# One multiplication for two buckets: pairing one-hot buffers in a four-layer graph network kernel

## The chip, the cores and the metric

The kernel runs on one core of a Trainium2 chip. The metric is the time of one execution on the device in microseconds (us). The engines of a core run side by side, each through its own queue in order: PE multiplies matrices (PEld is its loading of weights), DVE is the vector engine, ACT the scalar engine, POOL the general one, and SP issues transfers. They wait for each other through semaphores.

## The reference

Sixteen graphs of 1024 nodes with 128 features each go through four layers. The adjacency is sparse: an entry is there with a chance of about 1.6%, plus the diagonal. Each layer adds to `x`:

```python
x = x + L0(relu(layernorm(x)), adj, adj)   # degrees, neighbours by adj transposed, linear, relu
x = x + L1(relu(layernorm(x)), adj)        # mean of neighbours, linear, leaky relu
x = x + L2(relu(layernorm(x)), adj)        # scores on edges, two rounds
x = x + L3(relu(layernorm(x)), adj)        # attention by softmax
```

The change is in L2. A round of it, of which there are two, is this (`x` is a local name here):

```python
a = x @ We1[l, :D];  b = x @ We1[l, D:]
h = relu(a[:, :, None, :] + b[:, None, :, :] + be1[l])
scores = sigmoid((h @ We2[l]).squeeze(-1) + be2[l])
messages = (adjacency * scores) @ x
# then a two-layer update of [x, messages], a residual, a layer norm
```

Scores are needed only where the adjacency isn't zero, and the kernel computes them only there.

## The kernel before, in words

The 1024 nodes are 8 tiles of 128. A *bucket* is a pair of tiles (t, u): 28 off the diagonal and 8 on it. The edges of a bucket get *slots*: 320 in a bucket off the diagonal, 480 on it, laid out in blocks of 128 (3 or 4 blocks; `ck`). Buckets are worked in 9 *groups* of four (`GROUPS`, Q = 4): two groups of diagonal buckets, seven of others. A group off the diagonal goes in both directions (`nd` = 2), a diagonal one in one.

For each bucket `build` makes four one-hot matrices in 8-bit floats: `on` and `om` (node by slot, for gathering) and their transposes `onT` and `omT` (slot by node, for scattering). It does so from counts, ranks and comparisons: `far` on ACT (line 816), `on` on DVE (line 820), a transpose through PE (line 829), `onT` on ACT (line 861), a product with the ranks on PE (line 865), `omT` by a comparison on DVE (line 869), another transpose, `om` on ACT (line 877). They live in a pool of their own, `hot`, in buffers handed round: 8 per kind for diagonal buckets, 30 for the other 28. They are built once per graph and read in both rounds.

A round of L2 (`round`) takes the groups in turn. For each bucket and direction `gather` fetches both nodes' features into slots by one-hot products (line 1008, PE), and splits the relu into a high half on ACT (line 1024) and a low half on DVE (line 1025). `dots` reduces them to one score per slot (line 1041). At the end of a group, `ends` applies a tanh to all of its scores, and then, beside the next group's gathers, `scores` turns them so that slots lie on partitions (line 1074), splits them into two 16-bit halves held in one 32-bit word (`u`, lines 1079 to 1086), and multiplies every bucket's `onT` or `omT` with them: line 1098, one DVE instruction per bucket and direction, eight in a group off the diagonal, four in a diagonal one. The results, `val`, already lie two buckets to a buffer. `scatter` then multiplies the other transposed one-hot with `val` on PE (line 1120), four parts to a group, two (bucket, direction) products to a part off the diagonal; DVE multiplies the result with the adjacency (`upd`, line 1128), and `messages` sums it up on PE (line 1137).

Three streams of work are interleaved: the rounds of graph b (`main`), the last steps of graph b-1 (`last`, with the attention layer), and the first layers of graph b+1, at whose end stands its `build` (`first`). `weave` writes the program in the order of each stream's progress in estimated microseconds; a scheduler then sets the order on each engine by dependencies and priority. A one-hot buffer of graph b is free for graph b+1 once its last reader in the second round is done: a scatter or a multiplication of line 1098.

Of the kernel before, what the change touches and what calls it, by code (L numbers as in the profile page):

```python
# [11 lines left out]
FP8 = mybir.dt.float8e4  # L12
I32 = mybir.dt.int32
AF = mybir.ActivationFunctionType
OP = mybir.AluOpType
# [36 lines left out]
def tile_four_gnn_layers(  # L52
# [24 lines left out]
    P = 128  # L77
# [6 lines left out]
    J = P // G  # L84
    Q = T // NH
# [96 lines left out]
    def flat(t):  # L182
        return t.rearrange("p t d -> p (t d)")
# [266 lines left out]
    def slots(t, s):  # L450

        return (C_DIAG, CK_DIAG) if t == s else (C_OFF, CK_OFF)
# [77 lines left out]
    class Edges:  # L530
# [271 lines left out]
            nc.vector.tensor_reduce(top[:, 1:2], end[:, no:], axis=AX.X, op=OP.max)  # L802
            nc.vector.tensor_tensor(self.most, self.most, top, op=OP.max)

        def hot_tile(self, what, t, u, n, name):

            kind, bufs = ("d", T + MORE_DIAG) if t == u else ("o", len(OFF) + MORE_OFF)
            return self.hot.tile(
                [P, n], FP8, tag=f"{what}{kind}", name=f"{what}_{name}", bufs=bufs
            )  # L810

        def rows_hot(self, s, t, u, name):
# [22 lines left out]
        def build(self, s, has, name):  # L835

            s.on, s.onT, s.om, s.omT = {}, {}, {}, {}
            yield None  # L840
            for g, grp in enumerate(GROUPS):
                c, ck = slots(*grp[0])

                pr = self.a.one(f"pr_{name}_{g}").rearrange("p (k m) -> p k m", m=P)
                for i, tu in enumerate(grp):
                    b = INDEX[tu]
                    nc.tensor.matmul(
                        pr[:, i], self.low2, s.cnt[:, b : b + 1].to_broadcast([P, P]),
                        start=True, stop=False,
                    )  # L850
                    nc.tensor.matmul(pr[:, i], has[:, b], self.tri2, start=False, stop=True)
                rank = self.work.tile([P, Q, P], F16, tag="rank", name=f"rank_{name}_{g}")
                nc.scalar.activation(rank, pr, AF.Copy)
                yield 0.5
                for i, (t, u) in enumerate(grp):
                    nm = f"{name}_{t}_{u}"
                    on = self.rows_hot(s, t, u, nm)
                    yield 0.1
                    pn = self.turned(on, ck, f"pn_{nm}")
                    onT = self.hot_tile("onT", t, u, ck * P, nm)  # L860
                    nc.scalar.activation(onT, pn[:, : ck * P], AF.Copy, saturate=False)  # L861
                    yield 0.35
                    pq = self.a.one(f"pq_{nm}").rearrange("p (k m) -> p k m", m=P)
                    for k in range(ck):
                        nc.tensor.matmul(  # L865
                            pq[:, k], on[:, k * P : (k + 1) * P], rank[:, i], start=True, stop=True
                        )
                    omT = self.hot_tile("omT", t, u, ck * P, nm)
                    nc.vector.tensor_tensor(
                        omT.rearrange("p (k m) -> p k m", m=P), pq[:, :ck],  # L870
                        self.odd[t == u][:, :, None].to_broadcast([P, ck, P]),
                        op=OP.is_equal, saturate=False,
                    )
                    yield 0.35
                    pm = self.turned(omT, ck, f"pm_{nm}")
                    om = self.hot_tile("om", t, u, c, nm)
                    nc.scalar.activation(om, pm[:, :c], AF.Copy, saturate=False)  # L877
                    s.on[t, u], s.om[t, u] = on, om
                    s.onT[t, u], s.omT[t, u] = (
                        v.rearrange("p (k n) -> p k n", n=P) for v in (onT, omT)  # L880
                    )
                    yield 0.35
# [73 lines left out]
        class Group:  # L956
# [110 lines left out]
            def scores(self):  # L1067


                path, ck, per, name = self.path, self.ck, self.per, self.name  # L1070
                row = path.srow
                pt = path.bank("sc", f"pt_{name}")
                for k in range(ck):
                    nc.tensor.transpose(pt[:, k * P : (k + 1) * P], row[:, k * P : (k + 1) * P], ident)
                pt = pt[:, : ck * P].rearrange("p (c r) -> p c r", r=G)[:, :, :per]
                u = path.work.tile([P, CK_DIAG * J * 2], F32, tag="u", name=f"u_{name}")
                u = u[:, : ck * J * per]
                u2 = u.bitcast(F16).rearrange("p (c r h) -> p c r h", r=per, h=2)
                nc.scalar.activation(u2[:, :, :, 1], pt, AF.Copy, scale=S_SCALE)
                nc.vector.scalar_tensor_tensor(  # L1080
                    u2[:, :, :, 0], pt, S_SCALE, u2[:, :, :, 1], op0=OP.mult, op1=OP.subtract
                )
                if not self.diag:

                    again = u2[TAIL:, (ck - 1) * J :]
                    nc.vector.tensor_copy(again[:, :, :, 1], again[:, :, :, 0])
                u = u.rearrange("p (k g r) -> p k g r", g=J, r=per)
                self.val, self.ps = {}, [None] * self.nd
                for d in range(self.nd):
                    for i in range(Q):  # L1090
                        if i % 2 == 0:
                            pair = flat(path.m.scratch(f"val_{name}_{d}_{i}")).rearrange(
                                "p (d c n) -> p d c n", d=2, n=P
                            )
                        j = i * self.nd + d
                        right = (self.s.omT if d else self.s.onT)[self.grp[i]]
                        v = u[:, :, j % J, j // J : j // J + 1]
                        nc.vector.tensor_tensor(  # L1098
                            pair[:, i % 2, :ck], right[:, :ck], v.to_broadcast([P, ck, P]), op=OP.mult
                        )  # L1100
                        self.val[d, i] = pair[:, i % 2]

            def scatter(self, part):

# [281 lines left out]
    with ExitStack() as stack:  # L1386
        path = Edges(stack)
# [16 lines left out]
    with tc.If(full > 0):  # L1404
        with ExitStack() as stack:
            path = Pairs(stack)
# [36 lines left out]
```

## Time and profile before

| | |
|---|---|
| time, median of 3 runs | 5404.78 us (5400.31 to 5408.11) |
| span of the profiled run | 5411.4 us |
| granted clock of PE, mean share | 0.978 |
| HBM traffic | 446.44 MB read, 100.66 MB written, 101 GB/s |
| DVE, line 1025 (hid) | 1010.0 us in 2048 instructions |
| DVE, line 1128 (upd) | 349.0 us in 512 |
| DVE, line 869 (omT off the diagonal) | 247.6 us in 448 |
| PE idle until ACT's onT (line 861), before line 865 | 39.1 us, 55 times |
| PE idle until DVE's omT (line 869), before line 829 | 27.9 us, 39 times |

How to read it: the page gives the busy time of every engine, that is the time covered by at least one of its instructions; a group of instructions has its busy time, the mean length of one, and the idle time of the engine just before them with what ended it. The chain of work that ended last is followed back from the last instruction, from each to what released it; an engine's share of the chain is the part of the span in which the end depended on it. Instructions of one engine overlap a little, so starts and lengths are to be read apart.

### The profile page before, as it was taken

How to read it: one execution, taken by the hardware profiler on the slowest of the kernel's cores; microseconds unless marked ns; L12 is line 12 of the kernel's file. 1: busy time of each engine (PE TensorE's matmuls, PEld its weight loads, DVE VectorE, ACT ScalarE, POOL GpSimd, SP SyncE). 2: the span in 40 equal slices, each digit the busy share in tenths (PEclk: the TensorE clock that was granted, in tenths of full speed). 3: DMA queues.
4: the chain of work that ended last, by engine and by line, in shares of the span. 5: the costliest groups of instructions: out<-in, count | busy, mean ns of one | idle time of the engine just before them, and what ended most of it. 6: DMA issues, size and time to landing. Idle time of an engine off the chain costs nothing.

```text
span 5411.4 us, 113484 instructions
## 1 busy us (share of the span) xinstructions
PE 5012.4 (93%) x45109; PEld 3743.8 (69%) x45109; DVE 4288.8 (79%) x10567; ACT 3055.3 (56%) x6790; POOL 176.5 (3%) x137
## 2 busy tenths in 40 slices
PE   5999999999999999999999999999999999999986
PEld 4666767767776767767777677677767677677664
DVE  4776787877879788797877878778797787978876
ACT  4556464655646556465565656556465564655533
POOL 0000000000000000000000000000000000000000
PEclk8999999999999999999999999999999999999998
DMA  6242425243252423424234242432424334243121
GB/s 182 66 138 87 120 60 150 79 128 103 76 149 64 136 92 99 133 67 124 92 112 121 61 142 87 122 106 76 147 67 137 91 96 136 67 128 92 53 62 47
DMA packets 740139, 554.56 MB, mean 102 GB/s; under 512 B 32272, under 2 KB 686352, under 8 KB 739600
## 3 DMA queue, kind: packets, MB, share of 16 engines
q1 hardware_dynamic: 734496, 545.58, 33.6%
q8 instruction: 356, 5.83, 0.5%
q10 hardware_dynamic: 5104, 1.65, 0.1%
q14 instruction: 183, 1.50, 0.1%
HBM read 446.44 MB, written 100.66 MB: 101 GB/s over the span
## 4 chain that ended last, share of the span: by engine, by line
PE 61%; DVE 20%; ACT 10%; DMA 4%; POOL 2%; issue 2%; SPq 0%; ACTq 0%; POOLq 0%; DVEq 0%
PE pre L1008 15%; PE p L1120 7%; DVE val L1098 6%; PE nb L289 6%; PE msg L1137 5%; PE h L343 4%; PE hp L507 3%; PE bb L297 3%; PE sc L1041 3%; DVE hid L1025 3%; DMA at<-in_adj_dram 3%; PE pq L865 2%; PE pn L829 2%; POOL st L242 2%; ACT hid L1024 2%
## 5 line engine op out<-in xcount | busy, mean ns | idle before, releaser
L1024 ACT ACTIVATE hid<-pre 128x320 f16<-128x320 f32 (+1 forms) x2048 | 922.2, 456 | 713.5 <-PE pre L1008 679.5
L1025 DVE SCALAR_TENSOR_TENSOR hid<-pre,hid 128x320 f16<-128x320 f32 (+1 forms) x2048 | 1010.0, 505 | 262.7 <-ACT hid L1024 245.8
L1008 PEld LDWEIGHTS <-part 128*128 128x128 f16 x8192 | 752.7, 99 | 429.3 <-issue 211.4
L1008 PE MATMUL pre<-on,part 128*128 128x320 fp8e4 (+1 forms) x4096 | 966.6, 311 | 42.5 <-DVE hid L1025 32.3
L1008 PE MATMUL pre<-om,part 128*128 128x320 fp8e4 (+1 forms) x4096 | 979.0, 312 | 0.0
L1098 DVE TENSOR_TENSOR val<-onT,u 128x384 f32<-128x384 fp8e4 (+1 forms) x1152 | 603.3, 580 | 3.6
L1137 PE MATMUL msg<-upd,xf 128*128 128x128 f32 (+3 forms) x3008 | 591.8, 320 | 0.0
L1120 PE MATMUL p<-val,omT 128*128 128x128 f16 x6528 | 532.7, 219 | 31.6 <-DVE val L1098 27.2
L1120 PEld LDWEIGHTS <-omT 128*128 128x128 fp8e4 x6528 | 433.4, 96 | 109.6 <-issue 37.1
L1098 DVE TENSOR_TENSOR val<-omT,u 128x384 f32<-128x384 fp8e4 x896 | 442.7, 549 | 0.0
L1137 PEld LDWEIGHTS msg<-upd,xf 128*128 128x128 f32 x3008 | 411.6, 191 | 17.6 <-DVE upd L1128 0.9
L877 ACT ACTIVATE om<-pm 128x320 fp8e4<-128x320 f32 (+1 forms) x576 | 268.6, 466 | 274.5 <-PE pm L829 270.1
L1128 DVE SCALAR_TENSOR_TENSOR upd<-p,adj 128x512 f32<-128x512 f32 x512 | 349.0, 682 | 80.7 <-PE p L1120 76.7
L1120 PE MATMUL p<-val,onT 128*128 128x128 f16 x4480 | 370.9, 220 | 1.4 <-DVE upd L1128 1.4
L861 ACT ACTIVATE onT<-pn 128x384 fp8e4<-128x384 f32 (+1 forms) x576 | 298.4, 518 | 106.4 <-PE pn L829 98.4
L1062 ACT ACTIVATE srow<-sc,be_s,down 128x128 f32<-128x128 f32 (+2 forms) x512 | 256.3, 540 | 163.3 <-PE sc L1041 162.3
L507 PE MATMUL hp<-wh,e 128*128 128x129 f32 x2048 | 331.1, 287 | 16.7 <-DVE e L503 16.7
L1120 PEld LDWEIGHTS <-onT 128*128 128x128 fp8e4 x4480 | 305.2, 97 | 49.5 <-issue 14.9
L507 PEld LDWEIGHTS hp<-wh,e 128*128 128x128 f32 x2048 | 279.9, 195 | 51.5 <-issue 24.0
L1041 PE MATMUL sc<-hid,slide 128*32 128x320 f16 (+1 forms) x4096 | 272.4, 320 | 29.9 <-DVE hid L1025 28.5
L820 DVE TENSOR_SCALAR on<-far,wid 128x384 fp8e4<-128x384 f16 (+1 forms) x576 | 238.6, 427 | 60.0 <-PE pre L1008 52.2
L816 ACT ACTIVATE far<-iota_off,mid 128x384 f16<-128x384 f16 x448 | 275.6, 629 | 11.8 <-DVE on L820 11.3
(217 smaller groups left out, 8122.0 us busy)
## 6 DMA issues: line engine op xcount, KB each, us to landing
at<-in_adj_dram SPq DMA_DIRECT2D x128, 512.0 KB, 4.1
ct<-in_adj_dram SPq DMA_DIRECT2D x128, 512.0 KB, 4.5
adjT<-tn SPq DMA_DIRECT2D x128, 512.0 KB, 5.3
l<-adjT SPq DMA_DIRECT2D x128, 512.0 KB, 4.3
adj<-adjT SPq DMA_DIRECT2D x256, 256.0 KB, 3.5
a<-adjT SPq DMA_DIRECT2D x128, 384.0 KB, 3.2
adj<-adjT SPq DMA_DIRECT2D x448, 64.0 KB, 2.2
adj<-adjT SPq DMA_DIRECT2D x192, 128.0 KB, 2.9
```

Of the source, the lines that this page charges most:

```text
L289: nc.tensor.matmul(ps, mat[:, k], z[:, k], start=(k == 0), stop=(k == T - 1))
L507: nc.tensor.matmul(sums[:, t], e[:, i, t * P : (t + 1) * P], wh[:, k + i, : D + 1], start=False, stop=True, skip_group_check=True,)
L816: nc.scalar.activation(far[:, : ck * P], self.iota[t == u][:, : ck * P], AF.Abs, bias=s.mid[:, i : i + 1])
L861: nc.scalar.activation(onT, pn[:, : ck * P], AF.Copy, saturate=False)
L1008: nc.tensor.matmul(pre[:, :c], path.parts[node // Q][:, k, node % Q, v], hot[:, :c], start=(hot is on and k == 0), stop=(hot is om and k = ...
L1024: nc.scalar.activation(hid[:, 0, :c], pre[:, :c], AF.Relu)
L1025: nc.vector.scalar_tensor_tensor(hid[:, 1, :c], pre[:, :c], 0.0, hid[:, 0, :c], op0=OP.max, op1=OP.subtract)
L1041: ins = nc.tensor.matmul(self.sc[g * G : (g + 1) * G, : self.c], self.path.slide[:, self.l, G - 1 - r : 2 * G - 1 - r], self.hid[self.done ...
L1098: nc.vector.tensor_tensor(pair[:, i % 2, :ck], right[:, :ck], v.to_broadcast([P, ck, P]), op=OP.mult)
L1120: nc.tensor.matmul(self.ps[d][:, i], left[:, k], halves[:, k, :, h], start=(k, h) == terms[0], stop=(k, h) == terms[-1],)
L1128: nc.vector.scalar_tensor_tensor(upd, self.ps[d], S_SCALE, self.adj[:, d * Q : (d + 1) * Q], op0=OP.add, op1=OP.mult,)
L1137: nc.tensor.matmul(self.msg[h][:, (lo - h * Q) * P : (hi - h * Q) * P], self.xf[mb // Q][:, mb % Q], up, start=False, stop=True, skip_grou ...
```

## The change

`onT` and `omT` of two neighbouring buckets of a group get one buffer of twice the width (the `pair`), with half as many buffers in the pool; both buffers are taken at the first bucket of the two. As `val` already lay in pairs, one DVE instruction can now multiply the scores of two buckets into the one-hots of both: a loop over pairs takes the place of the loop over buckets, and the score operand gets one more dimension, with a step from one bucket's column to the next one's. What each bucket computes is unchanged. It is for having half as many DVE instructions of this kind, each of twice the size.

```diff
-        def hot_tile(self, what, t, u, n, name):
+        def hot_tile(self, what, t, u, n, name, both=1):
             kind, bufs = ("d", T + MORE_DIAG) if t == u else ("o", len(OFF) + MORE_OFF)
             return self.hot.tile(
-                [P, n], FP8, tag=f"{what}{kind}", name=f"{what}_{name}", bufs=bufs
+                [P, both * n], FP8, tag=f"{what}{kind}", name=f"{what}_{name}", bufs=bufs // both
             )
...
-                    onT = self.hot_tile("onT", t, u, ck * P, nm)
+                    if i % 2 == 0:
+                        pair = {
+                            what: self.hot_tile(what, t, u, ck * P, nm, 2).rearrange(
+                                "p (i k n) -> p i k n", i=2, n=P
+                            )
+                            for what in ("onT", "omT")
+                        }
+                        s.pairs[t, u] = pair
+                    onT, omT = (flat(pair[what][:, i % 2]) for what in ("onT", "omT"))
...
-                    omT = self.hot_tile("omT", t, u, ck * P, nm)
...
-                for d in range(self.nd):
-                    for i in range(Q):
-                        if i % 2 == 0:
-                            pair = flat(path.m.scratch(f"val_{name}_{d}_{i}")).rearrange(
-                                "p (d c n) -> p d c n", d=2, n=P
-                            )
-                        j = i * self.nd + d
-                        right = (self.s.omT if d else self.s.onT)[self.grp[i]]
-                        v = u[:, :, j % J, j // J : j // J + 1]
+                nd = self.nd
+                for d in range(nd):
+                    for i in range(0, Q, 2):
+                        pair = flat(path.m.scratch(f"val_{name}_{d}_{i}")).rearrange(
+                            "p (i c n) -> p i c n", i=2, n=P
+                        )
+                        right = self.s.pairs[self.grp[i]]["omT" if d else "onT"]
+                        j = i * nd + d
+                        v = u[:, :, j % J : j % J + nd + 1 : nd, j // J : j // J + 1]
                         nc.vector.tensor_tensor(
-                            pair[:, i % 2, :ck], right[:, :ck], v.to_broadcast([P, ck, P]), op=OP.mult
+                            pair[:, :, :ck], right, v.rearrange("p k i o -> p i k o").to_broadcast(
+                                [P, 2, ck, P]
+                            ), op=OP.mult,
                         )
-                        self.val[d, i] = pair[:, i % 2]
+                        for h in range(2):
+                            self.val[d, i + h] = pair[:, h]
```

## The prediction

> **What bounds the kernel now.** I read the page first: the shares of the engines, then the chain that ended last, then the costliest groups.
>
> ```profile
> PE 5012.4 (93%) x45109; PEld 3743.8 (69%) x45109; DVE 4288.8 (79%) x10567; ACT 3055.3 (56%) x6790; POOL 176.5 (3%) x137
> ...
> PE 61%; DVE 20%; ACT 10%; DMA 4%; POOL 2%; issue 2%; SPq 0%; ACTq 0%; POOLq 0%; DVEq 0%
> PE pre L1008 15%; PE p L1120 7%; DVE val L1098 6%; PE nb L289 6%; PE msg L1137 5%; PE h L343 4%; PE hp L507 3%; PE bb L297 3%; PE sc L1041 3%; DVE hid L1025 3%; DMA at<-in_adj_dram 3%; PE pq L865 2%; PE pn L829 2%; POOL st L242 2%; ACT hid L1024 2%
> ...
> L1098 DVE TENSOR_TENSOR val<-onT,u 128x384 f32<-128x384 fp8e4 (+1 forms) x1152 | 603.3, 580 | 3.6
> L1120 PE MATMUL p<-val,omT 128*128 128x128 f16 x6528 | 532.7, 219 | 31.6 <-DVE val L1098 27.2
> ...
> L1098 DVE TENSOR_TENSOR val<-omT,u 128x384 f32<-128x384 fp8e4 x896 | 442.7, 549 | 0.0
> ```
>
> The matrix engine (PE) carries 61% of the chain, the vector engine (DVE) 20%. Neither is the bound throughout. Line 1098, which the change rewrites, is 603.3 + 442.7 = 1046 us of DVE in 2048 instructions, and 6% of the chain, that is some 325 us of 5411: about a third of what it runs counts, two thirds lie under other work. It waits for almost nothing (3.6 us of idle before it). The matrix engine waits for it rarely: 27.2 us in all.
>
> How it runs is in the timeline of DVE, in the part of a batch where the next batch's one-hots are built (columns: start, length, instructions; several alike are merged):
>
> ```profile
> 2707.11 0.17 DVE L1086 COPY u<-u 64x8 f16<-64x8 f16 x1
> 2707.32 0.56 DVE L869 TENSOR_TENSOR omT<-pq,odd_off 128x384 fp8e4<-128x384 f32 x1
> 2707.79 1.95 DVE L1098 TENSOR_TENSOR val<-onT,u 128x384 f32<-128x384 fp8e4 x4
> 2709.66 1.96 DVE L1098 TENSOR_TENSOR val<-omT,u 128x384 f32<-128x384 fp8e4 x4
> 2711.54 0.55 DVE L869 TENSOR_TENSOR omT<-pq,odd_off 128x384 fp8e4<-128x384 f32 x1
> 2712.00 0.88 DVE L1025 SCALAR_TENSOR_TENSOR hid<-pre,hid 128x320 f16<-128x320 f32 x2
> ```
>
> Eight multiplications stand in one block of 3.83 us (2707.79 to 2711.62), and the hid of line 1025, on which the gathers of PE depend, comes after them. That block is what is on the chain. The reader is to see the starts: four instructions take 2709.66 - 2707.79 = 1.87 us, 468 ns each, although one lasts 549. Each overlaps the next by some 80 ns, so the price of one more instruction is less than its length suggests. The table of windows tells where DVE is short:
>
> ```profile
> 2675.00:2700.00 25.00, 24.13 (x257) 18.89 (x256) 24.24 (x57) 16.70 (x42) 0.00 (x0) 1.00 0.22 65
> 2700.00:2725.00 25.00, 24.65 (x262) 18.46 (x260) 23.74 (x57) 19.24 (x46) 0.00 (x0) 1.00 0.22 65
> ...
> 2450.00:2475.00 25.00, 24.86 (x235) 19.23 (x233) 18.99 (x43) 14.52 (x34) 0.00 (x0) 1.00 0.50 145
> 2475.00:2500.00 25.00, 24.83 (x229) 19.21 (x227) 18.26 (x45) 12.66 (x30) 0.00 (x0) 1.00 0.57 172
> ```
>
> (PE, weight loads, DVE, ACT.) In the build part both PE and DVE are nearly full, 24.1 to 24.7 and 23.7 to 24.2 of 25 us; in the other part PE is full and DVE has a quarter free.
>
> **What the Trainium skill says.** "VectorE: DVE Perf Modes", section on the TRN2 errata, gives a float32 tensor_tensor (N + 151) / 0.96 ns: 557 for 384 elements, 691 for 512. The trace agrees (549 and 684). The same section says that the latency is exposed between instructions, and that one large tile pays it once: this is what the change is after. Its table of perf modes holds a float32 tensor_tensor at one element per cycle, so merging can win only the fixed part; (684 - 550) / 128 = 1.05 ns per element here agrees. "Perfetto Trace Analysis" warns in its opening that matmul busy time says little since matmuls are pipelined. Here too: one line-1120 matmul lasts 219 ns but 6528 of them are busy for 532.7 us, 82 ns each. So 93% is no proof that PE is full.
>
> **The change part by part.**
> - *Removed:* 1024 of the 2048 instructions of line 1098. 224 groups of slots off the diagonal go from 8 to 4, 64 diagonal ones from 4 to 2. The elements stay.
> - *Cost of a merged one:* the row of line 501, a DVE pass over 128x768 float32, has a mean of 952 ns, and 550 + 384 x 1.05 = 953 agrees: I take 952 (the skill's formula would give 957). For 1024 elements 684 + 512 x 1.05 = 1222. Start to start: 468 + 384 x 1.05 = 871 (or 468 + 400 = 868 with the 384 / 0.96 of the skill's formula); I take 868. The trace shows no pass that also strides over two score columns and two halves of the output; I price that at nothing, as the present one already repeats a score over a stride of zero. If it did cost, the other end is no merging gain at all.
> - *The block:* before 7 x 469 + 549 = 3.83 us; after 3 x 868 + 952 = 3.56 us; 0.27 us less. On 224 groups that is 60 us, on 64 diagonal ones 2 x 68 ns each, 9 us: 69 us of DVE (4288.8 to about 4220). By the lengths alone it would be 1024 x (2 x 549 - 952) = 150 us; the overlap takes more than half of it back.
> - *On the path:* 68 of every 2 x 469 = 938 ns of line 1098 go, 7.3%. Of the 325 us on the chain that is 24 us. The other 45 us of DVE lie beside PE.
> - *Where it ends:* the hid of line 1025 and the omT of line 869 queue behind the block; they start up to 0.27 us sooner, and the gathers of PE wait for hid. But PE then has less room in which to hide its own queue: it is close to full in all four windows. I keep two thirds of the 24 us: 16.
> - *A later first half:* the scatter's first part needs both buckets of a pair. Its first bucket's value is ready 952 - 549 = 0.40 us later, its second 469 + 549 - 952 = 0.07 us sooner. PE stands still for line 1098 48 times (27.2 us): at most 48 x 0.40 = 19 us if all are first buckets. As the part's ten matmuls (0.73 us at full pace) otherwise stop in the middle for the second bucket (0.91 us at 2478.88), the net is nearer 0.2 us, some 10 us at most and partly paid by others' slack. It is in the third that I took off.
> - *Buffers:* onT and omT hold two buckets per buffer, with half the buffers: 15 for 14 pairs off the diagonal (before 30 for 28 buckets), 4 for 4 on it. Bytes are unchanged. A pair is freed when its later bucket is; both are read in the same part of a scatter, so release moves by less than a part. No new instruction waits.
> - *Moved:* the scheduler sets the order anew. Comparing the order on each engine, the same PE instructions are there, but the build's transposes and ranks (lines 829, 865) stand 8 rows later in the mean, some 25 early in each build, and the gathers (line 1008) 5 rows earlier. A PE row is 5411 us / 74,643 rows = 73 ns, so that is 0.6 us, and 1.8 us early in a build. ACT and the DMA queue keep their instructions. I count it as zero: a build finishes well before the first round that reads it, and the gathers advanced go to the round that sets the end.
>
> Sum: 5404.8 - 16 = 5389 us.
>
> **The rivals.**
> 1. *The blocks on the chain shrink, and most of it reaches the end* (forecast): 5389, between 5380 (all 24 us) and 5394.
> 2. *Hidden anyway:* PE takes the place of DVE on the chain at once. For it: PE at 24 of 25 us in both stages and only 27.2 us of waiting for line 1098. Against it: 325 us of line 1098 on the chain. Time: 5395 to 5414, about 5402.
> 3. *DVE counts for more than the chain says:* in the build stage DVE is 95 to 97% busy, so a round's eight or nine groups there give their 0.27 us each in full (15 x 8 x 0.27 = 32 us), and the first round its share of the chain, about 12. Time: 5404.8 - 44 = 5361; the floor is all 69 us, 5336. Against it: the chain runs through PE in most of that stage.
> 4. *Slower:* the new order or the larger pieces cost more than is saved. Builds start 1.8 us later in 15 batches (27 us if nothing hides it), waits for first halves add up to 10, against 16 won: 5404.8 + 21 = 5426. For it: no wait of before leaves much room; in the build stage omT can now stand behind 0.87 us rather than 0.47. Against it: all this sits in a stream with other work.
>
> **How the numbers follow.** Forecast 0.43, hidden 0.22, more 0.15, slower 0.20. With 0.2% = 10.8 us the bounds are 5394 and 5415.6. The forecast lies below the lower in all but a few cases (0.39 faster, 0.04 same); hidden gives 0.20 same and 0.02 faster; more is all faster; of slower 0.18 is over the upper bound and 0.02 same. Sum: faster 0.56, same 0.26, slower 0.18. The range takes in the inner part of the third and fourth cases, 5355 to 5421, and leaves about a tenth out on each side.
>
> **What would show it.** Right: one group of 1024 instructions for the multiplication with 768-element forms at about 950 ns and starts 870 ns apart; DVE busy near 4220; its share of the chain a little under 6%; PE busy unchanged. Wrong: merged passes well over 1000 ns (the access pattern costs); DVE down by 69 us and the span unchanged (case 2); more idle time of PE before its scatters, or of PE and ACT in the build stage (case 4); a span down by over 40 us (case 3).

## The result, and the profile after

The changed kernel takes 5319.19 us (median of 4 runs, 5315.3 to 5325.15) against 5403.35 (5400.31 to 5408.11) for the kernel before: a ratio of 0.9844, 95% interval 0.9827 to 0.9861, 84 us less. The forecast was 5389 us, with a range down to 5355. The direction was right, the size about a fifth of what came.

The page of the changed kernel, in the lines that answer to those of before (line 1098 is now 1106, the scatter's 1120 is 1131):

```profile
PE 4977.0 (93%) x45109; PEld 3739.4 (70%) x45109; DVE 4216.4 (79%) x9543; ACT 3044.9 (57%) x6790; POOL 189.3 (4%) x137
...
PE 55%; DVE 22%; ACT 12%; DMA 5%; issue 3%; POOL 2%; SPq 0%; ACTq 0%; POOLq 0%; DVEq 0%
...
L1106 DVE TENSOR_TENSOR val<-onT,u 128x768 f32<-128x768 fp8e4 (+1 forms) x576 | 561.1, 1010 | 3.1
L1131 PE MATMUL p<-val,omT 128*128 128x128 f16 x6528 | 507.3, 219 | 23.4 <-DVE val L1106 13.4
...
L1106 DVE TENSOR_TENSOR val<-omT,u 128x768 f32<-128x768 fp8e4 x448 | 410.7, 950 | 0.0
```

DVE lost 72.4 us of busy time (4288.8 to 4216.4), yet the span of the profiled execution lost 88. So the removed DVE work alone, even if all of it had been on the path, does not give the gain. Of the 88 us, PE's busy time gave 35 (5012.4 to 4977.0) and its idle time the rest, though PE's instructions are the same. PE's share of the chain fell from 61% to 55%.

The timeline of DVE in the build part, at about the same place of a batch:

```profile
2668.17 0.17 DVE L1093 COPY u<-u 64x8 f16<-64x8 f16 x1
2668.37 0.49 DVE L1032 SCALAR_TENSOR_TENSOR hid<-pre,hid 128x320 f16<-128x320 f32 x1
2668.78 1.82 DVE L1106 TENSOR_TENSOR val<-onT,u 128x768 f32<-128x768 fp8e4 x2
2670.51 1.82 DVE L1106 TENSOR_TENSOR val<-omT,u 128x768 f32<-128x768 fp8e4 x2
2672.25 0.55 DVE L876 TENSOR_TENSOR omT<-pq,odd_off 128x384 fp8e4<-128x384 f32 x1
```

Two passes take 2670.51 - 2668.78 = 1.73 us, 865 ns from start to start, and the block is 3.55 us (before 3.83). And there is a hid between `u` and the block that did not stand there in the stretch shown of before: the order is another one. The windows, of the same two parts of a batch (PE, weight loads, DVE, ACT):

```profile
2634.00:2659.00 25.00, 23.89 (x246) 18.77 (x245) 23.77 (x49) 18.79 (x47) 0.00 (x0) 1.00 0.23 65
2659.00:2684.00 25.00, 24.68 (x259) 18.13 (x259) 23.63 (x53) 17.54 (x43) 0.00 (x0) 1.00 0.21 62
2409.00:2434.00 25.00, 24.87 (x212) 17.89 (x211) 20.37 (x42) 15.48 (x36) 0.00 (x0) 1.00 0.35 105
2434.00:2459.00 25.00, 24.60 (x229) 19.75 (x229) 18.09 (x38) 12.14 (x29) 0.00 (x0) 1.00 0.63 188
```

They look as before: in these stretches what was won does not show in how full an engine is. Over the whole kernel it shows in what PE waits for. First the kernel before, then the changed one, from the view of waits (us in total, times, longest):

```profile
PE pq L865 <- ACT onT L861: 39.1, 55, 1.5
...
PE pre L1008 <- DVE hid L1025: 32.3, 51, 2.8
PE sc L1041 <- DVE hid L1025: 28.5, 22, 1.8
...
PE pm L829 <- DVE omT L869: 27.9, 39, 1.7
...
PE p L1120 <- DVE val L1098: 27.2, 48, 1.5
```

```profile
PE pre L1015 <- DVE hid L1032: 32.5, 52, 1.5
PE pm L829 <- DVE omT L876: 30.2, 50, 1.0
...
PE p L1131 <- DVE val L1106: 13.4, 47, 0.8
...
PE pq L873 <- ACT onT L869: 11.1, 30, 0.6
...
PE sc L1048 <- DVE hid L1032: 10.7, 14, 1.4
```

These five sum to 155 us before and 98 after; all of PE's waits fell from 357.5 to 306.6 us. Most of that fall is not at the rewritten line: the waits for `onT`, which ACT makes by an unchanged instruction, went from 39.1 to 11.1 us. Shorter DVE work could do that, or another order; both changed.

### The profile page after: what moved, and what is told of

Same layout as the page of the kernel before. It is cut to its first block, busy times and chain, and to the rows that moved or that the text cites. A ratio compares the mean times of both kernels' runs of the same rounds, so it can differ in the third digit from the quotient of the medians.

```text
span 5323.4 us, 112270 instructions
## 1 busy us (share of the span) xinstructions
PE 4977.0 (93%) x45109; PEld 3739.4 (70%) x45109; DVE 4216.4 (79%) x9543; ACT 3044.9 (57%) x6790; POOL 189.3 (4%) x137
## 4 chain that ended last, share of the span: by engine, by line
PE 55%; DVE 22%; ACT 12%; DMA 5%; issue 3%; POOL 2%; SPq 0%; ACTq 0%; POOLq 0%; DVEq 0%
PE pre L1015 14%; PE p L1131 7%; DVE val L1106 7%; PE nb L289 6%; PE msg L1148 5%; PE bb L297 3%; PE sc L1048 3%; DVE hid L1032 3%; DMA at<-in_adj_dram 3%; PE h L343 3%; PE hp L507 3%; ACT hid L1031 2%; PE pq L873 2%; PE pn L829 2%; DMA a<-adjT 2%
## 5 line engine op out<-in xcount | busy, mean ns | idle before, releaser
L1015 PE MATMUL pre<-on,part 128*128 128x320 fp8e4 (+1 forms) x4096 | 985.2, 310 | 42.7 <-DVE hid L1032 32.5
L1015 PE MATMUL pre<-om,part 128*128 128x320 fp8e4 (+1 forms) x4096 | 962.9, 309 | 0.0
L1106 DVE TENSOR_TENSOR val<-onT,u 128x768 f32<-128x768 fp8e4 (+1 forms) x576 | 561.1, 1010 | 3.1
L1131 PE MATMUL p<-val,omT 128*128 128x128 f16 x6528 | 507.3, 219 | 23.4 <-DVE val L1106 13.4
L1106 DVE TENSOR_TENSOR val<-omT,u 128x768 f32<-128x768 fp8e4 x448 | 410.7, 950 | 0.0
```

Of the source, the lines that this page charges most:

```text
L1015: nc.tensor.matmul(pre[:, :c], path.parts[node // Q][:, k, node % Q, v], hot[:, :c], start=(hot is on and k == 0), stop=(hot is om and k = ...
L1106: nc.vector.tensor_tensor(pair[:, :, :ck], right, v.rearrange("p k i o -> p i k o").to_broadcast([P, 2, ck, P]), op=OP.mult,)
L1131: nc.tensor.matmul(self.ps[d][:, i], left[:, k], halves[:, k, :, h], start=(k, h) == terms[0], stop=(k, h) == terms[-1],)
```

## The experiments

**The parts of the change, with the order on the engines held.** The scheduler sets the order anew for every program, so a comparison of two kernels always compares two orders. To separate them, a kernel can be held to another's order: for each engine, every instruction gets an edge to the one that stands ahead of it in the other program (shortened below). The edge fixes the order of issue alone and is to add no wait. In the traces of e2 and e3 no matmul, no ACT instruction and no DVE instruction but the multiplications themselves stands elsewhere than in the program whose order they follow. No kernel was held to its own order to measure that the edges cost nothing.

```diff
+        for a, b in zip(order, order[1:]):
+            tc.add_manual_dep(b, a.name, DependencyInfo(NoSync, DATA), reason="order")
```

Where a merged pass takes the place of two single ones, it stands at the place of the first.

e1 keeps the change's buffers and undoes the merging (shortened):

```diff
-                        nc.vector.tensor_tensor(pair[:, :, :ck], right, v..., op=OP.mult)
+                        for h in range(2):
+                            right = (self.s.omT if d else self.s.onT)[self.grp[i + h]]
+                            v = u[:, :, ((i + h) * nd + d) % J, ...]
+                            nc.vector.tensor_tensor(pair[:, h, :ck], right[:, :ck], v..., op=OP.mult)
```

> The buffers of the change (two buckets to a buffer) with the multiplications of before (2048, one per bucket); the scheduler's own order. Theory D (the shorter time of the DVE passes makes the gain, at more than its share of the chain): 5395 to 5410 us. Theory O (the new order on the engines makes it, the passes only the 16 to 24 us of the prediction): this order is a third one, so anything from 5330 to 5410. Theory B (the buffers make it): 5335 to 5345.

Measured: 5378.87 us, ratio to before 0.9961 (0.9947 to 0.9974). The same instructions as before, only the buffers are in pairs, and it is 20 us faster. That lies outside the ranges of B and D; that of O took in nearly anything. The multiplications last as long as before (552 ns, before 549 to 551); what the pairs do is to shift 52% of PE's matmuls to another place in its order, and to change when a one-hot buffer comes free. Which of the two makes the 20 us, e1 does not tell.

e2 is e1 with merged passes, all engines held to e1's order:

> The merged passes, with every engine held to the order that the kernel of e1 has. The one difference from e1 is the 1024 merged passes. Theory D: 65 to 85 us under e1. Theory O: 16 to 24 us under e1. Theory B: the same as O.

Measured: 5399.47 us, ratio 1.0005 (0.9997 to 1.0013): 21 us *slower* than e1, although DVE is busy 61 us less. No theory had that. The view of PE's waits, e1 and then e2:

```profile
PE p L1207 <- DVE val L1182: 21.5, 33, 1.5
```

```profile
PE p L1207 <- DVE val L1172: 62.1, 125, 1.9
PE tp L318 <- ACT xf L310: 38.7, 15, 5.2
```

PE stands still for the product of line 1098 125 times rather than 33, 41 us more, and it is now its greatest wait (the next one is as in e1, 38.5 us there). In this order the scatter stands where the first of two single passes was ready; by the prediction's estimate the merged one is ready 0.4 us later. e5 puts this reading to the test.

e3 is the reverse: single passes, all engines held to the order of the changed kernel.

> The buffers of the change, 2048 single multiplications, every engine held to the order of the changed kernel. Theory D: 5385 to 5405 us (the gain is gone). Theory O: 5335 to 5345 (the gain stays but for the passes' 16 to 24). Theory B: 5335 to 5345 as well, and e1 with it.

Measured: 5364.38 us, ratio 0.9934 (0.992 to 0.9947), between the ranges of D and O. So of the 84 us, 35 stay with the new order and the paired buffers, which e3 does not separate, and 0.9934 - 0.9844 = 0.9%, 49 us, go with the passes (by the two intervals some 37 to 61). As e3 and the changed kernel have one order, their waits can be set side by side. In e3:

```profile
PE pre L1079 <- DVE hid L1096: 49.5, 95, 1.9
...
PE pm L888 <- DVE omT L940: 40.7, 65, 1.4
...
PE pq L935 <- ACT onT L931: 10.7, 27, 0.6
...
PE p L1207 <- DVE val L1182: 0.4, 1, 0.4
```

In the changed kernel these are 32.5, 30.2, 11.1 and 13.4 us. That is the mechanism of the prediction, both ways: with merged passes PE waits less for hid and omT, which queue behind the block, and its scatter waits longer for the first value. The wait for onT is as short with single passes: its fall from 39.1 us came with the order and the pairs, not with the merging. Matched matmul by matmul, some 25 of the 36 us between the two profiles arise within 100 matmuls of one of a build's, which is half of the time, and 11 in the rest. The chain of e3:

```profile
PE 43%; DVE 34%; ACT 14%; DMA 4%; issue 3%; POOL 2%; SPq 0%; ACTq 0%; POOLq 0%; DVEq 0%
DVE val L1182 14%; PE pre L1079 12%; DVE hid L1096 5%; PE nb L348 4%; PE p L1207 4%; PE sc L1112 3%; PE bb L356 3%; PE msg L1224 3%; ACT hid L1095 3%; PE h L402 2%; ACT srow L1133 2%; DMA at<-in_adj_dram 2%; PE hp L566 2%; DVE omT L940 2%; PE pq L935 2%
```

In an order laid out for shorter passes, the single ones carry 14% of the chain, 750 us. 7.3% of that, by the prediction's own rule, is 55 us, near the 49 measured. It would be tempting to say that the rule was right and only the 6% of the kernel before the wrong share. The weavings below do not bear that out.

e4 has the merged passes with DVE, ACT and the DMA queue held to the order of before; PE's order is free. (All engines in the order of before were not tried.)

> The merged passes and their buffers, with DVE, ACT and the DMA queue held to the order of the kernel before; PE's order is the scheduler's and differs from that of before by 2.3 rows in the mean. Theory D: 5320 to 5340 us. Theory O: 5380 to 5390. Theory B: 5320 to 5345.

Measured: 5395.48 us, ratio 0.9994 (0.9987 to 1.0): no gain, outside the ranges of all three theories. DVE's busy time fell to 4220.4 us, and its idle time for PE's ranks (omT waiting for pq) rose from 56.5 to 105.2 us. Most of what was saved on DVE became waiting on DVE.

e5 and e6 tell which engine's order spoils e2. e5 frees PE alone, e6 holds PE alone.

> As e2 (merged passes, order of e1) but PE's order alone is left to the scheduler; DVE, ACT and the DMA queue stay held to the order of e1. Theory P (e2 lost because PE's scatters stand where the first single value was ready, 0.4 us before the merged one is; a PE order made for the merged pass mends it): 5340 to 5365 us, with PE's idle time until line 1098's value back from 62.1 us to under 30. Theory A (PE's order alone is not enough, all engines have to be set anew): 5380 to 5400.

> As e2, but only PE is held to the order of e1; DVE, ACT and the DMA queue are left to the scheduler. Theory P: still 5385 to 5405, PE's idle time until the value over 45 us. Theory A: between, 5360 to 5385.

Measured: e5 5361.86 us, 0.9917 (0.99 to 0.9934), by the ratios 48 us better than e2 and 24 better than e1 (which ran on another chip), with PE's wait for the product at 11.4 us: as theory P had it. e6 5513.92 us, 1.0202 (1.0185 to 1.0219), far worse than either theory allowed:

```profile
PE tn L814 <- ACT tn L815: 58.3, 40, 3.0
PE pre L1080 <- DVE hid L1097: 54.3, 101, 3.6
PE p L1208 <- DVE val L1173: 50.9, 109, 1.7
```

Here all kinds of waits grew, also those that have nothing to do with the change (`tn`, the transposes of the first layer): DVE and ACT were laid out for a PE that issues otherwise. So by these two runs orders have to fit each other; the same order of PE goes with 5399 us in e2 and 5514 in e6.

**How far does a mere change of order carry?** `MAIN_US` is an estimate by which the streams are woven; another value changes no instruction.

```diff
-MAIN_US = 184.0
+MAIN_US = 180.0
```

> The kernel before with one number of the weaving changed (MAIN_US 180 for 184): the same instructions in another order (80% of PE's instructions stand elsewhere). Theory G (the gain belongs to the merged passes in an order made for them): 5375 to 5410. Theory L (the order of before was merely a poor one, and any redrawing gains): 5320 to 5370 is as likely as 5400.

> The changed kernel with MAIN_US 180: the same instructions in another order. Theory G: 5305 to 5340, some 60 to 90 us under the run of before with 180. Theory L: 5350 to 5400, or within 30 us of the run of before with 180.

> The kernel before with MAIN_US 188: the same instructions in a third order of the weaving. Theory L (the order of before was a poor one, and e7's 5331 is what this instruction set usually takes): 5320 to 5360 us. Theory G' (orders of the single passes scatter over 5330 to 5405, those of the merged ones lie below): anywhere in 5330 to 5405.

> The changed kernel with MAIN_US 188. Theory L: within 5 to 30 us under the run of before with 188 (the passes alone). Theory G': 5305 to 5335 whatever the run of before with 188 gives.

> The kernel before with MAIN_US 176. Theory L: 5320 to 5360 us. Theory G': anywhere in 5330 to 5405.

> The changed kernel with MAIN_US 176. Theory L: within 5 to 30 us under the run of before with 176. Theory G': 5305 to 5335.

> The kernel before with MAIN_US 182. Theory M (the merged passes are worth some 55 us in the mean, orders scatter by some 60 for either kernel): 5330 to 5480. Theory C (they are worth the chain's share, 16 to 24, and the pairs so far were lucky): the same.

> The changed kernel with MAIN_US 182. Theory M: 20 to 90 us under the run of before with 182. Theory C: from 20 us over to 55 under it, as likely over as 40 under.

> The kernel before with MAIN_US 186. Both theories: 5330 to 5480.

> The changed kernel with MAIN_US 186. Theory M: 20 to 90 us under the run of before with 186. Theory C: from 20 us over to 55 under it.

Measured (medians in us; the two kernels of a new weaving on one chip; the ratio of each to the kernel before at 184 in brackets, all intervals within 0.0017 of it; the share of the chain that line 1098 has with single passes, and PE's waits summed, from the profiles):

| MAIN_US | single passes | merged passes | difference | chain share, single | PE's waits, single and merged |
|---|---|---|---|---|---|
| 176 | 5423.82 (1.0035) | 5354.09 (0.9907) | -70 | 6% | 398, 315 |
| 180 | 5331.22 (0.9866) | 5321.91 (0.9845) | -9 | 8% | 311, 286 |
| 182 | 5356.38 (0.9912) | 5330.01 (0.9864) | -26 | 9% | 323, 316 |
| 184 (given) | 5403.35 | 5319.19 (0.9844) | -84 | 6% | 358, 307 |
| 186 | 5440.61 (1.0070) | 5386.51 (0.9965) | -54 | 7% | 397, 359 |
| 188 | 5475.19 (1.0136) | 5423.64 (1.0038) | -52 | 7% | 431, 374 |

Four things follow. The same instructions take from 5331 to 5475 us, 2.7%, by their order alone: more than the change brings. The kernel before with 180 comes within 12 us of the changed one, without any change to its work (theory L in its strong form, that all weavings but the given one take 5320 to 5360, fell with 5424, 5441 and 5475). And merged passes are faster in all six weavings, by 49 us in the mean with a standard error of 11 (95% interval of six differences: 20 to 78). The 84 us of the given weaving, which raised the question, is the largest of the six; the other five have a mean of 42 us (12 to 72). No weaving tried beat the changed kernel at 184.

The fourth is on the prediction's rule, 7.3% of what line 1098 has on the chain. For the six kernels with single passes it gives 24 to 36 us, and it does not go along with the gain: most at 182, where the line has 9% of the chain and merging brings 26 us, least at 184, where it has 6% and merging brings 84. The chain of single passes at 182:

```profile
PE pre L1008 13%; DVE val L1098 9%; PE p L1120 6%; PE msg L1137 5%; PE nb L289 5%; DVE hid L1025 4%; PE h L343 3%; DMA at<-in_adj_dram 3%; PE sc L1041 3%; PE bb L297 3%; PE hp L507 2%; PE pq L865 2%; ACT hid L1024 2%; DVE omT L869 2%; POOL st L242 1%
```

Of the theories none came through whole. G fell with 5331 at 180, G' with 5424 and 5475 (single) and with 5354 and 5424 (merged); L's few us for the passes fell at 176 and 188, with 70 and 52. M and C were to be told apart by 182 and 186, and both differences, 26 and 54 us, lie within the ranges of both. Only over all six is a worth of 16 to 24 us at the lower edge of the interval.

Where merging gains 50 us or more, PE's waits fall by 38 to 84 us in sum. In the pair at 176 it is those behind DVE's queue, before and then after:

```profile
PE pm L829 <- DVE omT L869: 56.3, 78, 1.7
PE pre L1008 <- DVE hid L1025: 50.5, 75, 1.8
PE pq L865 <- ACT onT L861: 45.2, 71, 1.7
```

```profile
PE pq L873 <- ACT onT L869: 23.0, 84, 0.6
...
PE pre L1015 <- DVE hid L1032: 18.2, 40, 1.4
...
PE pm L829 <- DVE omT L876: 6.0, 12, 0.8
```

omT, hid and onT were waited for 152 us, and now 47. The last is made on ACT; as e3 shows, its wait can fall without merging, so what of the 105 us belongs to the passes is open. At 180 the waits fall by 25 us as well, but PE's busy time rises from 4976.0 to 4990.7, and little is left.

## Why the prediction was right in part and wrong

*What bounds the kernel; the merged pass.* Right. A merged pass lasts 951 and 950 ns (forecast 952), 1218 over 1024 elements (1222), starts are 865 ns apart (868), the block is 3.55 us (3.56), DVE is busy 4216.4 us (4220). The pattern with two more strides costs nothing (951 ns, against 952 for the pass of line 501). That the fixed part is paid once, as the Trainium skill says in "VectorE: DVE Perf Modes", section on the TRN2 errata, holds here from start to start: two single passes take 2 x 468 ns, a merged one 865, to within 3 ns of the forecast 868.

*"Of the 325 us on the chain that is 24 us", "I keep two thirds".* Wrong in size: this is the first term that failed. It priced the passes at 16 us, 24 at most; in the order that the changed kernel got they are worth 49 (e3). The mechanism named, hid and omT sooner behind the block, is the one that the waits of e3 and of the changed kernel show. The step that failed is to take the share of one order's chain as the price of the passes: with e1's order, where the line has 6% of the chain too, merging lost 21 us (e2), and over six weavings share and gain do not go together. Over the weavings merging is worth 49 us in the mean, but its interval, 20 to 78, does not exclude 24; that the term was too small is shown for the given weaving, not for every order.

*"I count it as zero", of the moved instructions.* Wrong, and about as large an error: e3 puts 35 us on the new order together with the pairs, e1 20 us on another, and the weavings, in which buffers and instructions stay the same, spread single passes over 144 us. I had compared the orders, seen shifts of 0.6 us in the mean and 1.8 early in a build, and taken the size of a shift for the size of its effect. In these runs the distance does not tell the effect: e1's order and the changed kernel's each move about half of PE's matmuls, and single passes take 5379 us in the one and 5364 in the other.

*"A later first half", at most some 10 us.* Right in its mechanism, and its bound held only where PE's order was redrawn: e2, with the order of e1, waits 41 us more. In the trace of the changed kernel a median of 28 matmuls stands between the turned scores and the first scatter (24 to 25 before), and the wait fell to 13.4 us.

*The rivals.* The third, that DVE counts for more than its share of the chain, came nearest for the passes: 44 us, 32 of them in the build stage, against 49 measured, of which about two thirds arise there. But it took the whole DVE saving (5336) as its floor; the order and the pairs went below that. The second, hidden anyway, is what e4 does: 68 us less DVE work and no time. The fourth, that order and larger pieces cost more than they save, is what e2 does against e1. All were true of some order, and the forecast had no way to tell which order it would get. The range should have taken in a term of some tens of us either way for that alone.

*The checks named.* PE's busy time was to stay; it fell by 35 us. Merging is not needed for that: e1, with single passes, has 4977.7 us. Part of it can be the clock (last section). The chain's share of the multiplication was to fall a little; it rose to 7%.

*Open:* why the given weaving suited merged passes so much better than single ones. That an order can do as much is shown by the weavings; which of the places of 45,109 matmuls matter, and what the buffers add, is not.

## What to carry to other kernels

Where a scheduler sets the order, the same instructions can spread over some percent; measure that spread with a change that alters no instruction, before a small gain is believed or forecast. Compare a change in several orders, or with the order held, and hold it to one that was made for the new instruction lengths: in the old one a shorter instruction on a side engine may win nothing, and a longer one may stall the engine behind it. An engine's share of the chain says where to look; here it did not price the work, not even in the order that it was read from.

## What was not expected of the hardware

The granted clock of PE went with the order: 0.978 in the profile of before, 0.983 in that of the changed kernel, 0.985 for single passes woven at 180, and 0.976 at 188. Runs of the kernel before differ in it too. Fitted chip by chip (58 runs on four chips), a run takes 1.5 to 3.0 us less for each 0.001 more; over the 0.005 between the two profiles that is 7 to 15 us of the 84. A slope does not tell which of the two follows from the other.

The traces show which comes first. The clock is recorded there as full or half, in stretches of 3.41 us or a multiple. One place in the profile of before (PE busy, weight loads, DVE, ACT, POOL, then the clock):

```profile
2174.91:2178.33 3.42, 3.42 (x30) 2.54 (x29) 2.74 (x12) 1.25 (x4) 0.00 (x0) 1.00 0.56 200
2178.33:2181.74 3.41, 1.55 (x14) 1.02 (x13) 1.41 (x6) 2.57 (x7) 1.01 (x1) 1.00 0.51 156
2181.74:2185.15 3.41, 3.41 (x21) 3.26 (x19) 3.41 (x10) 0.40 (x1) 0.00 (x0) 0.50 0.65 160
2185.15:2188.57 3.42, 3.42 (x39) 2.68 (x38) 2.75 (x9) 0.26 (x1) 0.00 (x0) 1.00 0.59 172
```

PE waits 1.9 us and is busy for 1.55 of 3.41 us; in the next stretch the clock is at half, and then full again. Counted over the profile of before, without its first 200 and last 250 us: after stretches at full clock with PE busy for less than 40%, the next was at half in 11 of 11 cases, with 40 to 70% in 18 of 68, above that in none of 1337. (In the changed kernel: 11 of 11, 8 of 44, none of 1350. For single passes at 188: 13 of 13, 4 of 60, but 5 of 1349, which stay unexplained.) So the clock mostly follows PE's waits, and a wait can cost more than its own length. Fewer waits then mean a higher clock: half clock came in 29 such places before, in 19 after. At most half of the time at half clock is lost; 0.022 of 5411 us before and 0.017 of 5323 after make a difference of some 29 us, an upper estimate of what went this way. e3's profile has the clock of the changed kernel's, 0.983, so little of the passes' 49 us can be of this kind.
